# A memory-writing product kernel: VectorE's products in four stretches with fewer waits and counts, even shares, one more border

## The chip, the cores and the metric

The kernel runs on one core of a Trainium2 chip. The time is the device time of one execution in microseconds; a kernel's figure is the median over its runs. Engines are named as the profile names them: DVE is VectorE, ACT is ScalarE, SP is SyncE, POOL is GpSimd. A "q" after an engine's name (DVEq) means its sequencer. A "DMA engine" is one of the core's 16 engines that move the data; a "transfer" is one DMA instruction, whose rows are shared out over all 16.

## The reference

For each row of a 4096 x 256 float32 matrix, all products of two of its elements x_i x_j with i <= j, in the order of the upper triangle's rows:

```python
dot = jnp.einsum('bi,bj->bij', inputs, inputs)
iu, ju = jnp.triu_indices(256)
return dot[:, iu, ju]          # 4096 x 32896 float32
```

The input is 4.19 MB and the output 538.97 MB, so the kernel reads little and writes much.

## The kernel before

Each of the 128 partitions has 32 rows of the input. Two of them (`REPEAT`) are worked on together, so there are 16 groups. A group's 32896 output columns are cut into three thirds (`PIECES`), at columns 10944 and 21920. A piece is one third of one group: 128 partitions x 2 rows x about 10970 columns, and one transfer of 11.2 MB writes it out. Six pieces (two groups) make one pass of the loop (`PASS`), and there are eight passes. Output pieces alternate between two places in the on-chip memory (`PLACES`), so a piece can be computed only when the transfer of the piece two before it has landed.

In a piece, row i of the triangle is the stretch x_i * x_i, ..., x_i * x_255. The piece's first rows go to ScalarE (L206, one activation with a scale for each row i and each of the two input rows), the others to VectorE (L185, one multiplication for both input rows, and mostly for two rows i at once, m = 2 in `vector_ops`, L43). A multiplication with m = 2 writes one element too many, which the next row of the triangle overwrites; therefore that next product must come after it. `split` (L71) chooses how many rows ScalarE gets: it moves rows over until VectorE's planned time is within the third's budget, a number of nanoseconds for each output column of the two rows (`BUDGETS`, L22: 0.95, 0.80 and 0.85), or ScalarE would have more than VectorE.

`interleave` (L57) cuts VectorE's part of a block into two halves and takes products from them in turn. In `vector` (L172) each product goes through `Work.add` (L144): it counts one up on VectorE's own semaphore, and it waits until all products but the last one issued have finished. A product therefore waits for the one two places before it in the order.

The first two pieces are computed ahead of the loop ("ahead"). The very first is cut in blocks at `FIRST` (L23), 512, 1536 and 3584 columns, and each block is sent out as soon as both engines have it; four transfers make up this piece. All other pieces are one block and one transfer. After a block VectorE waits for its own last product and then signals `v_done`; ScalarE waits for its own last instruction and signals `a_done` (L215).

In the loop VectorE first takes `free` of the place (L178, through `take`, L135), which the transfer two pieces before raised by 16 when it landed, then raises `go`, which ScalarE takes (L202). SyncE (L218) takes `v_done` and `a_done` and issues the transfer (L226). All transfers are issued by SyncE, in order. At the start it also issues the three loads of the input (L247).

Of the kernel before, what the change touches and what calls it, by code (L numbers as in the profile page):

```python
# [9 lines left out]
AF = mybir.ActivationFunctionType  # L10
ALU = mybir.AluOpType
# [3 lines left out]
REPEAT = 2  # L15
PIECES = 3
PLACES = 2
PASS = 6
AHEAD = 2


BUDGETS = [0.95, 0.8, 0.85]  # L22
FIRST = [512, 1536, 3584]  # L23


def even_borders(lo: int, hi: int, pieces: int) -> list[int]:
# [30 lines left out]
def interleave(block: list) -> list:  # L57


    half = len(block)  # L60
    while half and len(vector_ops(block[:half])) > len(vector_ops(block[half:])):
        half -= 1
    a, b = vector_ops(block[:half]), vector_ops(block[half:])
    return [op for k in range(max(len(a), len(b))) for ops in (a, b) for op in ops[k : k + 1]]


def vector_time(block: list) -> float:
# [15 lines left out]
def window(ap: bass.AP, free: list) -> bass.AP:  # L83
    return bass.AP(ap.tensor, ap.offset, [list(ap.ap[0]), *free])


@with_exitstack
def kernel(
    ctx: ExitStack, tc: tile.TileContext, x: bass.AP, out: bass.AP
):  # L90

    nc = tc.nc
    n, d = x.shape
    width = out.shape[1]
    each, groups = REPEAT * d, n // (P * REPEAT)
    rounds = PASS // PIECES
    passes = groups // rounds
    assert n % (P * REPEAT) == 0 and width == d * (d + 1) // 2 and width % UNIT == 0
    assert PASS % PLACES == 0 and AHEAD == PLACES and PASS % PIECES == groups % rounds == 0  # L110
    borders = even_borders(0, width, PIECES)
    spans = list(zip(borders, borders[1:]))
    slot = max(b - a for a, b in spans)

    x_in = x.rearrange("(p g) d -> p (g d)", p=P)
    x_out = out.rearrange("(p h q r) c -> h q p r c", p=P, q=rounds, r=REPEAT)

    pool = ctx.enter_context(tc.tile_pool(name="all", bufs=1))
    xt = pool.tile([P, passes, rounds * each], F32, name="x")

    xv = pool.tile([P, each + 1], F32, name="xv")
    xa = pool.tile([P, each], F32, name="xa")
    places = [pool.tile([P, REPEAT, slot], F32, name=f"o{k}") for k in range(PLACES)]
    ctx.enter_context(tc.tile_critical())  # L124

    def semaphore(name: str):
        return ctx.enter_context(nc.semaphore(name))

    free = [semaphore(f"free{k}") for k in range(PLACES)]
    head, v_done, a_done, go = (semaphore(s) for s in ("head", "v_done", "a_done", "go"))  # L130
    loads = [0, each, groups // 2 * each, groups * each]
    loaded = [semaphore(f"loaded{k}") for k in range(len(loads) - 1)]

    def take(engine, sem, value: int):
        engine.wait_ge(sem, value).then_inc(sem, -value)  # L135

    class Work:

        def __init__(self, engine, name: str):
            self.engine, self.sem, self.count, self.marked = engine, semaphore(name), 0, 0

        def add(self, ins, back: int, mark: bool = True):  # L144
            if self.count > back:
                ins._wait_ge(self.sem, self.count - back)
            if mark:
                ins.then_inc(self.sem, 1)
                self.count += 1

        def end(self):
            return self.engine.wait_ge(self.sem, self.count)

        def restart(self):
            self.engine.sem_inc(self.sem, -self.count)  # L155
            self.count = 0

    v, a = Work(nc.vector, "v_own"), Work(nc.scalar, "a_own")

    def x_of(h, q: int) -> bass.AP:  # L160
        return xt[:, bass.ds(h, 1), q * each : (q + 1) * each].rearrange("p o d -> p (o d)")

    def blocks(p: int, ahead: bool):

        lo, hi = spans[p % PIECES]
        cuts = [lo, *(FIRST if ahead and p == 0 else []), hi]
        for a, b in zip(cuts, cuts[1:]):
            block = runs(d, a, b)
            k = split(block, 0.0 if ahead else BUDGETS[p % PIECES] * REPEAT * (b - a))
            yield a - lo, b - lo, block[:k], block[k:], lo  # L170

    def vector(h, pieces: range, ahead: bool):  # L172
        for p in pieces:
            if p % PIECES == 0:
                v.add(nc.vector.tensor_copy(xv[:, :each], x_of(h, p // PIECES)), 0)  # L175
                v.end()
            if not ahead:
                take(nc.vector, free[p % PLACES], 16)  # L178
                nc.vector.sem_inc(go, 1)  # L179
            for _, _, _, block, lo in blocks(p, ahead):  # L180
                for (i, j, at, length), m in interleave(block):
                    at -= lo

                    v.add(
                        nc.vector.tensor_tensor(  # L185
                            places[p % PLACES][:, :, at : at + m * length],
                            window(xv[:, j:], [[d, REPEAT], [1, m], [1, length]]),
                            window(xv[:, i:], [[d, REPEAT], [1, m], [0, length]]),
                            ALU.mult,
                        ),  # L190
                        1,
                    )
                v.end().then_inc(v_done, 1)
        v.restart()

    def scalar(h, pieces: range, ahead: bool):
        for p in pieces:
            if p % PIECES == 0:
                a.add(nc.scalar.activation(xa, x_of(h, p // PIECES), AF.Copy), 0)  # L199
                a.end()  # L200
            if not ahead:
                take(nc.scalar, go, 1)  # L202
            for _, _, block, _, lo in blocks(p, ahead):
                todo = [(run, r) for run in block for r in range(REPEAT)]
                for (i, j, at, length), r in todo:
                    ins = nc.scalar.activation(  # L206
                        places[p % PLACES][:, r, at - lo : at - lo + length],
                        xa[:, r * d + j : r * d + j + length],
                        AF.Copy,
                        scale=xa[:, r * d + i : r * d + i + 1],  # L210
                    )
                if todo:
                    ins.then_inc(a.sem, 1)
                    a.count += 1
                a.end().then_inc(a_done, 1)  # L215
        a.restart()

    def sync(h, pieces: range, ahead: bool):  # L218
        for p in pieces:
            place = places[p % PLACES]  # L220
            parts = list(blocks(p, ahead))
            for lo, hi, *_, base in parts:
                take(nc.sync, v_done, 1)
                take(nc.sync, a_done, 1)
                to = x_out[bass.ds(h, 1), p // PIECES, :, :, base + lo : base + hi]
                nc.sync.dma_start(to.rearrange("o p r c -> p (o r) c"), place[:, :, lo:hi]).then_inc(  # L226
                    free[p % PLACES] if len(parts) == 1 else head, 16
                )

    def all_pieces(engine, pieces_of):  # L230
        pieces_of(0, range(AHEAD), True)
        if engine is not nc.sync:
            for sem in loaded[1:]:
                engine.wait_ge(sem, 16)
        kind = engine.engine
        with nc.Fori(
            0,
            passes,
            engines=OrderedEngineSet([kind]),
            head_slot={kind: 0} if engine is not nc.sync else {},  # L240
        ) as h:
            pieces_of(h, range(AHEAD, PASS), False)
            with engine.If(h < passes - 1):
                pieces_of(nc.s_assert_within(h + 1, 0, passes - 1), range(AHEAD), False)

    for (lo, hi), sem in zip(zip(loads, loads[1:]), loaded):
        nc.sync.dma_start(xt.rearrange("p h d -> p (h d)")[:, lo:hi], x_in[:, lo:hi]).then_inc(sem, 16)  # L247
    nc.vector.memset(xv[:, each:], 0.0)  # L248
    for engine in (nc.vector, nc.scalar):
        engine.wait_ge(loaded[0], 16)  # L250

    take(nc.gpsimd, head, 16 * (len(FIRST) + 1))
    nc.gpsimd.sem_inc(free[0], 16)
    for engine, pieces_of in ((nc.vector, vector), (nc.scalar, scalar), (nc.sync, sync)):
        all_pieces(engine, pieces_of)
    for k in range(PLACES):
        take(nc.sync, free[k], 16)
    for sem in loaded:
        take(nc.sync, sem, 16)
# [27 lines left out]
```

## Time and profile before

| what | value |
|---|---|
| median of 4 runs | 1273.57 us (1273.53 to 1273.59) |
| profiled execution, its own time | 1273.72 us |
| its span, first to last instruction | 1271.7 us |
| VectorE busy | 72% |
| ScalarE busy | 48% |
| DMA written, mean rate | 538.97 MB, 427 GB/s |
| transfers of the output | 51, issued between 6.2 and 1237.5 us |
| SyncE's waits for the two engines | 1231.2 us in 54 waits |

The span is the time from the first to the last instruction of the profile; 2.0 us of the execution lie outside it. In the profile's rows of instruction groups, the columns are line, engine and operation, output and input with their shapes, the count; then busy time and mean duration of one; then the idle time of the engine just ahead of these instructions, and what ended most of it. In the timeline the columns are start, duration, engine, line, operation, shapes and count, with the idle time ahead in brackets. In the rows of stretches the columns are the stretch, the granted clock, busy time and count of each engine, again the clock, the busy share of the DMA engines and their rate.

### The profile page before, as it was taken

The numbers are of one execution on the slowest core, as the hardware profiler recorded it, in microseconds if no ns is written. First come the engines' busy times: TensorE is split into PE (matmuls) and PEld (weight loads), VectorE is DVE, ScalarE is ACT, GpSimd is POOL, SyncE is SP. The second block draws the span as 40 slices with busy tenths as digits, with TensorE's granted clock in tenths as the row PEclk, the third lists the DMA queues.
The fourth block names the chain that finished last, engine by engine and source line by source line (L and its number), as shares of the span: only waits on it lengthen the run. The fifth ranks groups of instructions, "written<-read, shape, count | busy, mean of one in ns | idle before, by whom it ended". The sixth has DMA issues, their size and how long they took to land. (4 is left out here: it accounts for less than half of the span.)

```text
span 1271.7 us, 4308 instructions
## 1 busy us (share of the span) xinstructions
DVE 915.4 (72%) x1712; ACT 606.4 (48%) x1837; POOL 0.2 (0%) x4
## 2 busy tenths in 40 slices
DVE  8767786777768776687757877578776787677860
ACT  8725535254363543635337352473524635156350
POOL 0000000000000000000000000000000000000000
DMA  9999999999999999999999999999999999999998
GB/s 381 435 429 431 439 423 439 422 440 425 435 439 424 437 424 437 423 440 428 435 419 442 419 441 420 431 429 419 442 420 441 420 440 421 420 441 421 440 420 356
DMA packets 14310, 543.21 MB, mean 427 GB/s; under 512 B 864, under 2 KB 864, under 8 KB 1504
## 3 DMA queue, kind: packets, MB, share of 16 engines
q1 hardware_dynamic: 14304, 543.17, 99.3%
q14 instruction: 6, 0.05, 0.0%
HBM read 4.19 MB, written 538.97 MB: 427 GB/s over the span
## 5 line engine op out<-in xcount | busy, mean ns | idle before, releaser
L185 DVE TENSOR_TENSOR o<-xv 128x736 f32<-128x736 f32 (+61 forms) x1695 | 908.5, 624 | 311.6 <-DVEq L135 311.0
L206 ACT ACTIVATE o<-xa 128x198 f32<-128x198 f32 (+44 forms) x1820 | 595.0, 420 | 621.1 <-ACTq L135 620.6
L175 DVE COPY xv<-x 128x512 f32 (+1 forms) x16 | 6.8, 427 | 9.1 <-DVEq L155 4.2
L199 ACT ACTIVATE xa<-x 128x512 f32 (+1 forms) x16 | 10.1, 630 | 5.1 <-ACTq L155 3.4
L199 ACT ACT_TABLE_LOAD x1 | 1.3, 1283 | 4.1 <-DMA x<-in_r_inputs_dram 4.1
L248 DVE MEMSET xv<- 128x1 f32 x1 | 0.1, 59 | 1.0 <-SPq L124 1.0
L274 POOL MEMSET const-bfloat16-1.0<- 128x1 bf16 x1 | 0.1, 102 | 0.0
L274 POOL MEMSET const-uint8-127<- 128x1 uint8 x1 | 0.1, 102 | 0.0
L274 POOL MEMSET const-float32-1.0<- 128x1 f32 x1 | 0.1, 99 | 0.0
L274 POOL MEMSET const-float32-0.0<- 128x1 f32 x1 | 0.1, 98 | 0.2 <-issue 0.2
## 6 DMA issues: line engine op xcount, KB each, us to landing
out_dram<-o SPq DMA_DIRECT2D x32, 10976.0 KB, 33.1
out_dram<-o SPq DMA_DIRECT2D x15, 10944.0 KB, 30.7
out_dram<-o SPq DMA_DIRECT2D x1, 7360.0 KB, 19.9
x<-in_r_inputs_dram SPq DMA_DIRECT2D x1, 2048.0 KB, 12.3
out_dram<-o SPq DMA_DIRECT2D x1, 2048.0 KB, 11.5
x<-in_r_inputs_dram SPq DMA_DIRECT2D x1, 1792.0 KB, 6.8
out_dram<-o SPq DMA_DIRECT2D x1, 1024.0 KB, 9.9
out_dram<-o SPq DMA_DIRECT2D x1, 512.0 KB, 9.3
```

The lines of the kernel that those rows point to most:

```text
L175: v.add(nc.vector.tensor_copy(xv[:, :each], x_of(h, p // PIECES)), 0)
L185: nc.vector.tensor_tensor(places[p % PLACES][:, :, at : at + m * length], window(xv[:, j:], [[d, REPEAT], [1, m], [1, length]]), window(xv ...
L199: a.add(nc.scalar.activation(xa, x_of(h, p // PIECES), AF.Copy), 0)
L206: ins = nc.scalar.activation(places[p % PLACES][:, r, at - lo : at - lo + length], xa[:, r * d + j : r * d + j + length], AF.Copy, scale=x ...
L248: nc.vector.memset(xv[:, each:], 0.0)
L274: nc = _bacc.Bacc("TRN2", target_bir_lowering=False, num_devices=1)
```

## The change

`BUDGETS` becomes 0.85 for all three thirds, and `FIRST` gets a fourth border at 6400, so the first piece goes out in five transfers. `interleave` cuts VectorE's part into four stretches (`SETS`) of about equal numbers of products and takes one from each in turn. With each product it returns the place of the product in the same stretch that has to be finished before it, if that one has m = 2. `vector` adds a wait only where such a product isn't covered by an earlier wait. A wait is for the product two places before or for the one that is needed, whichever is later in the order; and only products that some wait is for, and the block's last, count on the semaphore. ScalarE signals `a_done` with its block's last instruction instead of after a wait for itself, except in the last third of a group, where the wait stays. `go` is no longer taken after each piece: ScalarE's first instruction of a piece waits for the running number of turns, and the semaphore is set back at the end of a call.

```diff
+SETS = 4
...
-BUDGETS = [0.95, 0.8, 0.85]
-FIRST = [512, 1536, 3584]
+BUDGETS = [0.85, 0.85, 0.85]
+FIRST = [512, 1536, 3584, 6400]
...
 def interleave(block: list) -> list:
-    half = len(block)
-    while half and len(vector_ops(block[:half])) > len(vector_ops(block[half:])):
-        half -= 1
-    a, b = vector_ops(block[:half]), vector_ops(block[half:])
-    return [op for k in range(max(len(a), len(b))) for ops in (a, b) for op in ops[k : k + 1]]
+    sets, k = [], 0
+    for left in range(SETS, 0, -1):
+        share = -(-len(vector_ops(block[k:])) // left)
+        end = k
+        while end < len(block) and len(vector_ops(block[k : end + 1])) <= share:
+            end += 1
+        if left == 1:
+            end = len(block)
+        sets.append(vector_ops(block[k:end]))
+        k = end
+    order, last = [], {}
+    for step in range(max(map(len, sets))):
+        for s, ops in enumerate(sets):
+            if step < len(ops):
+                order.append((*ops[step], last.get(s)))
+                last[s] = len(order) - 1 if ops[step][1] == 2 else None
+    return order
...
     def vector(h, pieces: range, ahead: bool):
...
-                for (i, j, at, length), m in interleave(block):
+                order = interleave(block)
+                counted, waits = {len(order) - 1}, {}
+                for k, (*_, before) in enumerate(order):
+                    if before is not None and before > max(waits.values(), default=-1):
+                        waits[k] = max(before, k - 2)
+                        counted.add(waits[k])
+                number = {k: done + 1 + c for c, k in enumerate(sorted(counted))}
+                for k, ((i, j, at, length), m, _) in enumerate(order):
...
+                    if k in waits:
+                        ins._wait_ge(v_own, number[waits[k]])
+                    if k in counted:
+                        ins.then_inc(v_own, 1)
+                done += len(counted)
+                nc.vector.wait_ge(v_own, done).then_inc(v_done, 1)
+        nc.vector.sem_inc(v_own, -done)
...
     def scalar(h, pieces: range, ahead: bool):
...
-            if not ahead:
-                take(nc.scalar, go, 1)
...
-                if todo:
-                    ins.then_inc(a.sem, 1)
-                    a.count += 1
-                a.end().then_inc(a_done, 1)
+                if not ahead:
+                    turns += 1
+                    todo[0]._wait_ge(go, turns)
+                if not todo:
+                    nc.scalar.sem_inc(a_done, 1)
+                elif (p + 1) % PIECES:
+                    todo[-1].then_inc(a_done, 1)
+                else:
+                    todo[-1].then_inc(a_own, 1)
+                    done += 1
+                    nc.scalar.wait_ge(a_own, done).then_inc(a_done, 1)
+        for sem, count in ((a_own, done), (go, turns)):
+            if count:
+                nc.scalar.sem_inc(sem, -count)
```

More of the change, by code (lines that the diff above doesn't have):

```diff
@@ L135, in take @@
         engine.wait_ge(sem, value).then_inc(sem, -value)
[L137 to L158, printed above, removed]
+    v_own, a_own = semaphore("v_own"), semaphore("a_own")
     def x_of(h, q: int) -> bass.AP:
@@ L172, in vector @@
     def vector(h, pieces: range, ahead: bool):
+        done = 0
         for p in pieces:
+            place = places[p % PLACES]
             if p % PIECES == 0:
-                v.add(nc.vector.tensor_copy(xv[:, :each], x_of(h, p // PIECES)), 0)
-                v.end()
+                ins = nc.vector.tensor_copy(xv[:, :each], x_of(h, p // PIECES))
+                if done:
+                    ins._wait_ge(v_own, done)
+                ins.then_inc(v_own, 1)
+                done += 1
+                nc.vector.wait_ge(v_own, done)
             if not ahead:
@@ L180, in vector @@
             for _, _, _, block, lo in blocks(p, ahead):
-                for (i, j, at, length), m in interleave(block):
-                    at -= lo
[L184 to L191, printed above, removed]
-                    )
@@ L193, in vector @@
-                v.end().then_inc(v_done, 1)
-        v.restart()
+                order = interleave(block)
[6 more added lines that the diff above has]
+                for k, ((i, j, at, length), m, _) in enumerate(order):
+                    at -= lo
+                    ins = nc.vector.tensor_tensor(
+                        place[:, :, at : at + m * length],
+                        window(xv[:, j:], [[d, REPEAT], [1, m], [1, length]]),
+                        window(xv[:, i:], [[d, REPEAT], [1, m], [0, length]]),
+                        ALU.mult,
+                    )
+                    if k in waits:
+                        ins._wait_ge(v_own, number[waits[k]])
+                    if k in counted:
+                        ins.then_inc(v_own, 1)
@@ L196, in scalar @@
+                done += len(counted)
+                nc.vector.wait_ge(v_own, done).then_inc(v_done, 1)
+        nc.vector.sem_inc(v_own, -done)
     def scalar(h, pieces: range, ahead: bool):
+        done = turns = 0
         for p in pieces:
+            place = places[p % PLACES]
             if p % PIECES == 0:
-                a.add(nc.scalar.activation(xa, x_of(h, p // PIECES), AF.Copy), 0)
-                a.end()
-            if not ahead:
-                take(nc.scalar, go, 1)
+                nc.scalar.activation(xa, x_of(h, p // PIECES), AF.Copy).then_inc(a_own, 1)
+                done += 1
+                nc.scalar.wait_ge(a_own, done)
@@ L203, in scalar @@
             for _, _, block, _, lo in blocks(p, ahead):
[L204 to L207, printed above, removed]
+                todo = [
+                    nc.scalar.activation(
+                        place[:, r, at - lo : at - lo + length],
                         xa[:, r * d + j : r * d + j + length],
@@ L211, in scalar @@
                     )
-                if todo:
-                    ins.then_inc(a.sem, 1)
-                    a.count += 1
-                a.end().then_inc(a_done, 1)
-        a.restart()
+                    for i, j, at, length in block
+                    for r in range(REPEAT)
+                ]
+                if not ahead:
[7 more added lines that the diff above has]
+                    todo[-1].then_inc(a_own, 1)
+                    done += 1
+                    nc.scalar.wait_ge(a_own, done).then_inc(a_done, 1)
+        for sem, count in ((a_own, done), (go, turns)):
+            if count:
+                nc.scalar.sem_inc(sem, -count)
     def sync(h, pieces: range, ahead: bool):
```

## The prediction

> **What bounds the kernel now.** I read the page's busy times first, then the DMA queues, the waits, the timeline of one pass and the last microseconds.
>
> ```profile
> span 1271.7 us, 4308 instructions
> ...
> DVE 915.4 (72%) x1712; ACT 606.4 (48%) x1837; POOL 0.2 (0%) x4
> ...
> q1 hardware_dynamic: 14304, 543.17, 99.3%
> ...
> L185 DVE TENSOR_TENSOR o<-xv 128x736 f32<-128x736 f32 (+61 forms) x1695 | 908.5, 624 | 311.6 <-DVEq L135 311.0
> L206 ACT ACTIVATE o<-xa 128x198 f32<-128x198 f32 (+44 forms) x1820 | 595.0, 420 | 621.1 <-ACTq L135 620.6
> ```
>
> The 16 DMA engines are full 99.3% of the span. VectorE idles 311 us and ScalarE 621 us, nearly all at L135, where they wait for a place to come free (VectorE) or for the go that follows it (ScalarE). So products are not what the end waits for; the output's transfers are. A change to the engines can gain only where the DMA is not full, or where the engines slow the DMA.
>
> The timeline of one pass shows the rhythm. VectorE starts a piece when the transfer two before it has landed on all 16 engines, so the distance from start to start is the transfer time of the slowest DMA engine.
>
> ```profile
> 1139.76 18.89 DVE L185 TENSOR_TENSOR o<-xv 128x468 f32<-128x468 f32 x60 [8.51 <-DVEq L135]
> 1139.79 18.39 ACT L206 ACTIVATE o<-xa 128x98 f32<-128x98 f32 x62 [13.53 <-ACTq L135]
> ...
> 1166.15 20.75 DVE L185 TENSOR_TENSOR o<-xv 128x996 f32<-128x996 f32 x22 [6.83 <-DVEq L135]
> 1166.21 5.66 ACT L206 ACTIVATE o<-xa 128x256 f32<-128x256 f32 x14 [7.19 <-ACTq L135]
> 1192.20 17.52 DVE L185 TENSOR_TENSOR o<-xv 128x768 f32<-128x768 f32 x24 [5.30 <-DVEq L135]
> 1192.23 12.49 ACT L206 ACTIVATE o<-xa 128x7 f32<-128x7 f32 x36 [20.37 <-ACTq L135]
> 1218.22 18.88 DVE L185 TENSOR_TENSOR o<-xv 128x468 f32<-128x468 f32 x60 [8.50 <-DVEq L135]
> ```
>
> The distances are 26.39, 26.05 and 26.02 us: longest where VectorE runs its 60 short products. The row at 1139.76 also has 18.89 us of work in 18.9 us of wall time: within a piece VectorE has no gap that dropping a wait could close.
>
> The end shows who is slow.
>
> ```profile
> 1264.00:1265.00 1.00, 0.00 (x0) 0.00 (x0) 0.00 (x0) 1.00 1.63 702
> 1265.00:1266.00 1.00, 0.00 (x0) 0.00 (x0) 0.00 (x0) 1.00 0.00 0
> 1266.00:1267.00 1.00, 0.00 (x0) 0.00 (x0) 0.00 (x0) 1.00 0.11 44
> 1267.00:1268.00 1.00, 0.00 (x0) 0.00 (x0) 0.00 (x0) 1.00 0.00 0
> 1268.00:1269.00 1.00, 0.00 (x0) 0.00 (x0) 0.00 (x0) 1.00 0.10 44
> ```
>
> The columns after the clock are DMA share and GB/s; a packet is counted in the slice in which it starts, so rows swing. From 1266 on one packet per slice is left, a single 43.9 KB one: one DMA engine of 16 is still working and the others are done. In the landing records 15 engines finish the last transfer by 1266.65 us and one at 1270.33. That one sets the end.
>
> I followed the landings through the run. From 770 to 1220 us the slow engine needs 26.37, 26.11 and 26.02 us for the transfers that fly while 60, 22 and 24 products are computed. The median engine, in the stretch where it waits for nothing (400 to 560 us), needs 26.03, 25.98 and 25.95. So the slow one loses 0.34, 0.13 and 0.07 us, 0.54 per three pieces. For the last transfer, beside which almost nothing is computed, the slow engine needs 25.95 us, as fast as the others. Its packets say the same: 1627 ns with idle engines, about 1650 with four products per packet, about 1665 with six or seven, about 1631 with two. So it is slowed by what the engines do, and it is the only one.
>
> **The change, part by part.**
>
> *Counts and waits on VectorE.* Counted out of the loops, the loop's three kinds of piece have 60, 22 and 24 products before, each of which counts on VectorE's semaphore and nearly all of which wait. After, they have 61, 20 and 26 products, of which 20, 7 and 9 count and 19, 6 and 8 wait. VectorE itself gains nothing that matters: it is full within a piece already, and a faster piece would only idle longer at L135. What can matter is the slow DMA engine. Two readings of the loss fit the trace. Per product it is 0.34/60 = 5.7 ns, 0.13/22 = 5.9 and 0.07/24 = 2.9: roughly a price for each product. ScalarE's 63, 14 and 36 instructions, which do not count, do not order it that way: a fit over the packets of the second half gives 4.7 ns for each VectorE product that starts in a packet and -0.1 for each ScalarE one. What a product has that a ScalarE instruction lacks is the count (and the wait). If the count is the price, the losses shrink with it: 0.34 x 20/60 = 0.11, 0.13 x 7/22 = 0.04, 0.07 x 9/24 = 0.03. Saved: 0.23 + 0.09 + 0.04 = 0.36 us per three pieces. From the landing of the first piece at about 40.5 us on there are 47 transfers, 15.67 threes: 15.67 x 0.36 = 5.6 us. The trace of before has no product without a count, so this has bounds from both sides: nothing (the product itself is the price; there are as many, 107 for 106), and 15.67 x 0.54 = 8.5 us (with counts this rare the slow engine falls into step with the others). I take 5.6, since the ScalarE rows, instructions without counts, are the nearest to a product without one.
>
> [...]
>
> *Even shares.* The first third's VectorE share falls with its budget, 20.75 x 0.85/0.95 = 18.6 us, and ScalarE gets 22 instructions for 14, 5.66 x 22/14 = 8.9 us. The second third goes to 17.52 x 0.85/0.80 = 18.6 and ScalarE to 12.49 x 32/36 = 11.1. The last third stays. Cost on the path: nothing. What hides it is the transfer in flight: SyncE issues the three transfers 7.9, 6.9 and 4.7 us before the slow engine has finished the one before (second, last, first third). The worst goes to about 6.9, the best to 6.8. Against the 15 others the first third is issued only 0.7 us ahead, which gives them a gap of about 0.5 us; that gap goes, and is worth nothing while the slow engine sets the end. If the cover were gone, each us would be paid in each of 47 transfers.
>
> *One more border.* Now the fourth transfer of the first piece is late:
>
> ```profile
> 21.57 0.37 SPq L226 DMA_DIRECT2D out_dram<-o  x1
> ```
>
> The third has its last packets end around 22, and the fourth's first packets come 0.1 to 0.6 us after them on the engines, 0.35 on average. With the border at 6400 the fourth has 2816 of the 7360 columns: VectorE and ScalarE took 10.2 us for the 7360 (11.2 to 21.4), so about 3.9 for these, and it is issued near 15.3, well ahead. The rest, 4544 columns, is issued near 21.6 as now, while 2816 columns are in flight for some 6.8 us. That takes away 0.35 us and adds one more packet per row: packets of 8192 B take 309 ns, of 29440 B 1093, so 6.7 ns of each don't scale with size, and 16 more per engine are 0.1 us. One more DMA on SyncE takes 0.4 us there, with nothing behind it. Net -0.2 us, between -0.5 and +0.1.
>
> *ScalarE's ends and the cumulative go.* ScalarE's last instruction counts for SyncE directly, without the wait for itself: some 0.05 us per piece under leads of 4.7 us and more. Nothing.
>
> *Sum* against the profiled execution, 1273.72 us (its span of 1271.7 and 2.0 around it): -5.6 -0.2 = 1267.9. That execution lies 0.15 above the median of the runs, 1273.57, so the forecast for a median is **1267.8**. The 0.15 also says that the loss is not one of the profiled execution alone.
>
> **Rivals.**
>
> *The product, not its count, slows the engine.* For it: the price per product holds about as well as the price per count, since before they are the same number, and packets with both engines busy are the worst. Against it: ScalarE's instructions cost next to nothing. A mixture in which every instruction of both engines and every count pay alike: before, 106 products, 112 ScalarE instructions and 106 counts in three pieces, 324; after, 107, 116 and 36, 259. That is a fifth less, 1.7 of the 8.5 us. Then only the border stays: 1273.4, or 1271.7 for the mixture.
>
> *The other DMA engines take over.* If the slow one falls wholly into step, the others' 77.96 us per three pieces set the end: 8.5 + 0.2 less, 1264.9. That is the far end of my forecast, not another sign.
>
> *VectorE gets slower: slower overall.* Four stretches in turn, and products without a wait, may cost each product more. It decides when a piece's products take over about 26 us, the transfer time. The last third has 61 products in 18.9 us and a lead of 6.9 us, so each would have to grow by 6.9/61 = 113 ns. At 125 ns the excess is 0.7 us in each of the 16 last thirds, 11 us: 1285. Against it: the smallest product now takes 153 ns all told, the waits look two products back before and after, and nothing in the rows shows a price of that kind.
>
> **How the numbers follow.** The counted-semaphore case has 0.50, no change (product, or nothing) 0.42, slower 0.08. Within 0.2%, 2.5 us, is about what a measurement of this kernel can tell from no change, so the mixture falls in the second. The range goes from 1264.6 (8.5 and the border's 0.5 off) up to 1273.7 (nothing off, the border at its worst, +0.1), which takes in the no-change case. The likeliest case's own range is 1264.6 to 1271.0. Chances: faster 0.50, same 0.42, slower 0.08.
>
> **What will show it.** Start-to-start distances of VectorE near 26.15, 26.02 and 25.98 for 26.39, 26.05, 26.02; a last DMA engine that ends within 1 to 2 us of the others, for 3.7; the fourth transfer issued near 15 us. If the 60-product distance stays at 26.4 with a third of the counts, the product is the price and my forecast is wrong by the whole 5.6. If VectorE's last third takes well over 19 us, the third rival is under way.

## The result, and the profile after

The changed kernel takes 1272.25 us (median, 1272.05 to 1272.52) against 1273.56 for the one before; the ratio is 0.999, with a 95% interval of 0.9985 to 0.9995. So it is faster by 1.3 us, a tenth of a percent: the sign of the forecast and about a quarter of its size.

The page of the changed kernel, the same parts as before:

```profile
span 1270.0 us, 4343 instructions
...
DVE 896.2 (71%) x1733; ACT 633.9 (50%) x1897; POOL 0.2 (0%) x4
...
q1 hardware_dynamic: 14576, 543.17, 99.4%
...
L189 DVE TENSOR_TENSOR o<-xv 128x752 f32<-128x752 f32 (+62 forms) x1716 | 889.3, 605 | 329.2 <-DVEq L148 328.4
L213 ACT ACTIVATE o<-xa 128x253 f32<-128x253 f32 (+58 forms) x1880 | 622.5, 434 | 591.5 <-DVEq L177 591.4
```

The engines' work has moved a little, from VectorE (908.5 to 889.3 us) to ScalarE (595.0 to 622.5), and both still idle for hundreds of microseconds until a place is free. The DMA is as full as before (99.4% of the span for 99.3). The timeline of one pass (start, duration, instruction group, idle before it):

```profile
1138.23 18.83 DVE L189 TENSOR_TENSOR o<-xv 128x468 f32<-128x468 f32 x61 [7.54 <-DVEq L148]
...
1164.58 18.55 DVE L189 TENSOR_TENSOR o<-xv 128x980 f32<-128x980 f32 x20 [6.85 <-DVEq L148]
...
1190.64 18.46 DVE L189 TENSOR_TENSOR o<-xv 128x776 f32<-128x776 f32 x26 [7.51 <-DVEq L148]
...
1216.66 18.82 DVE L189 TENSOR_TENSOR o<-xv 128x468 f32<-128x468 f32 x61 [7.55 <-DVEq L148]
```

The distances from start to start are 26.35, 26.06 and 26.02 us, where they were 26.39, 26.05 and 26.02. Only the one with the 61 short products has moved visibly, and by hundredths. The end, in stretches of 1 us (the first figure behind a stretch is its length in us; the granted clock stands only once, behind the busy times, and after it DMA share and GB/s):

```profile
1263.00:1264.00 1.00, 0.00 (x0) 0.00 (x0) 0.00 (x0) 1.00 0.10 44
1264.00:1265.00 1.00, 0.00 (x0) 0.00 (x0) 0.00 (x0) 1.00 0.10 44
1265.00:1266.00 1.00, 0.00 (x0) 0.00 (x0) 0.00 (x0) 1.00 0.00 0
1266.00:1267.00 1.00, 0.00 (x0) 0.00 (x0) 0.00 (x0) 1.00 0.10 44
```

One DMA engine is still alone at the end, longer than before: in the landing records the others finish at 1263.25 and it at 1268.69, 5.4 us apart for 3.7. The others have gained 3.4 us, which fits the first thirds no longer coming late for them, and it is worth nothing, as the slow engine sets the end.

For the experiments one number is read from each profile: the time of the slowest DMA engine from landing to landing, as a mean over the transfers from some 460 us on, for the second, last and first third. Its scatter from transfer to transfer is 0.01 to 0.04 us, over ten transfers of each kind. The transfer of a second third is in flight while the next last third is computed, so what is changed in the last third shows in the first of these three numbers. In the first 270 us or so of after, the engine that lands last shows no such price (its transfer beside 61 products takes 25.94 us), so it seems to be another one; the trace does not number the engines. "Products" are VectorE's, "counts" are increments of an engine's own semaphore by its products or instructions (ScalarE's one at the end of a block is left out), all for three pieces in the loop. The medians are of different sets of runs, in which the kernel before took 1273.41 to 1273.57 us, so one or two tenths between rows mean nothing.

| kernel | products | ScalarE instr. | counts | second, last, first third (us) | sum | median (us) |
|---|---|---|---|---|---|---|
| before | 106 | 112 | 106 | 26.375, 26.104, 26.025 | 78.504 | 1273.56 |
| after | 107 | 116 | 36 | 26.328, 26.089, 26.004 | 78.422 | 1272.25 |
| all count | 107 | 116 | 107 | 26.375, 26.111, 26.020 | 78.505 | 1273.60 |
| ScalarE counts | 107 | 116 | 149 | 26.396, 26.122, 26.036 | 78.554 | 1274.42 |
| twice the products | 163 | 116 | 17 | 26.457, 26.065, 26.002 | 78.524 | 1274.86 |
| no VectorE, last third | 46 | 116 | 16 | 26.172, 26.079, 26.004 | 78.255 | 1269.17 |
| little ScalarE, last third | 107 | 56 | 36 | 26.190, 26.087, 26.006 | 78.282 | 1270.11 |
| tiny products, last third | 107 | 116 | 36 | 26.336, 26.081, 26.003 | 78.420 | 1272.31 |
| budgets 1.00, 1.00, 0.95 | 117 | 74 | 39 | 26.308, 26.059, 25.983 | 78.351 | 1270.77 |

### The profile page after: what moved, and what is told of

Read it like the earlier page. It is cut to its first block, busy times and chain, and to the rows that moved or that the text cites. A ratio compares the mean times of both kernels' runs of the same rounds, so it can differ in the third digit from the quotient of the medians.

```text
span 1270.0 us, 4343 instructions
## 1 busy us (share of the span) xinstructions
DVE 896.2 (71%) x1733; ACT 633.9 (50%) x1897; POOL 0.2 (0%) x4
## 3 DMA queue, kind: packets, MB, share of 16 engines
q1 hardware_dynamic: 14576, 543.17, 99.4%
## 5 line engine op out<-in xcount | busy, mean ns | idle before, releaser
L189 DVE TENSOR_TENSOR o<-xv 128x752 f32<-128x752 f32 (+62 forms) x1716 | 889.3, 605 | 329.2 <-DVEq L148 328.4
L213 ACT ACTIVATE o<-xa 128x253 f32<-128x253 f32 (+58 forms) x1880 | 622.5, 434 | 591.5 <-DVEq L177 591.4
```

The source lines that it names most:

```text
L189: ins = nc.vector.tensor_tensor(place[:, :, at : at + m * length], window(xv[:, j:], [[d, REPEAT], [1, m], [1, length]]), window(xv[:, i:] ...
L213: nc.scalar.activation(place[:, r, at - lo : at - lo + length], xa[:, r * d + j : r * d + j + length], AF.Copy, scale=xa[:, r * d + i : r ...
```

## The experiments

"After" in the expectations is the changed kernel, and every edit is to it.

**All products count again.** Is the count the price?

```diff
+                counted = set(range(len(order)))
                 number = {k: done + 1 + c for c, k in enumerate(sorted(counted))}
```

> As after, but every product counts on VectorE's semaphore; waits, order, shares and borders stay. Before and after differ by 70 counts and 0.07 us of the slowest DMA engine's time per three pieces. Theory C (the count is the price): the slowest engine's three transfers are back at 78.50 us for 78.43, and the time at about 1273.4. Theory P (the product instruction itself is the price) or W (the work of the engines is): 78.43 and 1272.25 as after.

Measured: 1273.60 us (1273.38 to 1273.75), ratio to before 1.0001 (0.9992 to 1.001), and a sum of 78.505. The whole gain is gone again with nothing but the counts put back:

```profile
1139.61 18.81 DVE L190 TENSOR_TENSOR o<-xv 128x468 f32<-128x468 f32 x61 [7.58 <-DVEq L148]
1165.99 18.54 DVE L190 TENSOR_TENSOR o<-xv 128x980 f32<-128x980 f32 x20 [6.89 <-DVEq L148]
1192.07 18.46 DVE L190 TENSOR_TENSOR o<-xv 128x776 f32<-128x776 f32 x26 [7.54 <-DVEq L148]
```

VectorE's busy times are those of after to 0.02 us, so the counts cost VectorE nothing; the first distance is 26.38 us. 71 counts for 0.083 us are 1.17 ns each. The waits stay as few as in after, 33 in three pieces where nearly all of the 106 products of before waited, and nothing is left of the gain: it was the counts and not the waits.

**ScalarE counts each instruction.** If a count has a price, it should not matter who counts.

```diff
+                for ins in todo[:-1]:
+                    ins.then_inc(a_own, 1)
+                done += max(len(todo) - 1, 0)
...
+        nc.scalar.wait_ge(a_own, done)
```

> As after, but every ScalarE instruction counts on ScalarE's semaphore, 116 more counts per three pieces. Theory C at 1.0 ns a count: 0.12 us more per three transfers, time 1274.1. Theories P and W: 1272.25.

Measured: 1274.42 us (1274.24 to 1274.72), ratio 1.0008 (0.9999 to 1.0018). 113 counts more are 0.132 us: again 1.17 ns each (by the scatter, both figures are good to 0.1 or 0.2).

```profile
1140.10 18.81 DVE L189 TENSOR_TENSOR o<-xv 128x468 f32<-128x468 f32 x61 [7.62 <-DVEq L148]
...
1166.49 18.54 DVE L189 TENSOR_TENSOR o<-xv 128x980 f32<-128x980 f32 x20 [6.90 <-DVEq L148]
```

The distance is 26.39 us. Theory C is shown for the counts, on either engine.

**Without the border at 6400.**

```diff
-FIRST = [512, 1536, 3584, 6400]
+FIRST = [512, 1536, 3584]
```

> As after, without the border at 6400. If the border is worth what I gave it, the first piece lands 0.2 us later and the time is 1272.45 (0.1 less to 0.5 more at the ends). If the border is the whole of the gain, 1273.5.

Measured: 1272.27 us (1272.15 to 1272.38), ratio 0.9991 (0.9982 to 1.0). The medians are 0.02 us apart, but they are of different runs: against before in its own runs this kernel gains 1.15 us (from 1273.42) and after 1.31. So the border is worth 0.2 us at most, less than these runs can tell from nothing. In the landing records the first piece lands at 41.27 us with it and at 41.72 without, and the last engine ends at 1268.69 and 1268.85. It does what was foreseen in its place, as after issues the fourth transfer 6 us sooner than before:

```profile
15.61 0.37 SPq L245 DMA_DIRECT2D out_dram<-o  x1
```

**Twice the products, same columns.** Does the product itself have a price? In the loop's last thirds VectorE multiplies one row at a time.

```diff
-def interleave(block: list) -> list:
+def interleave(block: list, single: bool = False) -> list:
+    ops_of = (lambda b: [(r, 1) for r in b]) if single else vector_ops
...
-                order = interleave(block)
+                order = interleave(block, not ahead and p % PIECES == 2)
```

> As after, but in the loop's last thirds VectorE multiplies one row at a time, about 117 products for 61 with the same columns; only the block's last counts, none waits. Theory C: 19 counts fewer, the slowest engine's transfer beside the last third goes from 26.32 to 26.30 or less, time 1272 or less. Theory P: the loss of 0.34 us doubles, 26.65, and 16 of these make 1277.5. Theory W (bytes): 26.32, 1272.25.

Measured: 1274.86 us (1274.74 to 1274.97), ratio 1.0011 (1.0002 to 1.002). Neither C, which wants a gain, nor P at its full price.

```profile
1141.07 18.38 ACT L214 ACTIVATE o<-xa 128x98 f32<-128x98 f32 x62 [14.90 <-DVEq L178]
1141.12 22.52 DVE L190 TENSOR_TENSOR o<-xv 128x234 f32<-128x234 f32 x117 [7.54 <-DVEq L149]
...
1167.61 18.54 DVE L190 TENSOR_TENSOR o<-xv 128x980 f32<-128x980 f32 x20 [3.29 <-DVEq L149]
```

The distance is 26.49 us. 56 products more and 19 counts less make 0.129 us; with the counts at 1.17 ns a product costs 2.7. So the product has a price of its own, twice that of its count, and half of what I had put on both together. Of the time, 1.3 us are something else, a late start at the loop's first piece:

```profile
43.65 22.53 DVE L190 TENSOR_TENSOR o<-xv 128x234 f32<-128x234 f32 x117 [5.93 <-DVEq L149]
...
66.58 0.39 SPq L246 DMA_DIRECT2D out_dram<-o  x1
```

It is issued half a microsecond before the fifteenth engine lands the transfer before (67.11 us), and its own transfer takes 27.21 us in the landing records, for 25.95 in after. The price of a product is read from the later transfers and doesn't have this in it. That price leaves much of the loss without an owner, and ScalarE's instructions as the suspects. Theory E: every instruction of either engine and every count has its price.

**VectorE leaves the last third out.** In this run and the next two a part of the output is not computed; the added memset, once ahead of the loop, fills columns that no engine would write.

```diff
+                if not ahead and p % PIECES == 2:
+                    nc.vector.sem_inc(v_done, 1)
+                    continue
                 order = interleave(block)
...
+    nc.vector.memset(places[0][:, :, borders[1] :], 0.0)
```

> As after, but in the loop VectorE leaves its products of the last third out (that part of the output is not computed); ScalarE's 62 instructions stay. The runs so far give 1.17 ns a count and 2.7 ns a VectorE product. Theory E (every instruction and every count has its price, on the slowest DMA engine alone): 61 products and 20 counts less beside the second third's transfer are 0.19 us, 26.33 to 26.14, time 1269.2. Theory B (only both engines working at once slows it): 25.97, time 1266.5.

Measured: 1269.17 us (1269.09 to 1269.36), ratio 0.9967 (0.9954 to 0.998). That is theory E's time; its transfer time is 26.17 for the 26.14 expected, 2.2 ns for a product. Theory B (both engines at once) is out.

```profile
1136.02 18.38 ACT L216 ACTIVATE o<-xa 128x98 f32<-128x98 f32 x62 [14.93 <-DVEq L177]
...
1162.21 8.80 ACT L216 ACTIVATE o<-xa 128x256 f32<-128x256 f32 x22 [6.98 <-DVEq L177]
```

From start to start of ScalarE it is 26.19 us, for 26.36 in after (1138.17 to 1164.53).

**ScalarE leaves most of the last third out.**

```diff
-                    for i, j, at, length in block
+                    for i, j, at, length in (block[:1] if not ahead and p % PIECES == 2 else block)
...
+    nc.vector.memset(places[0][:, :, borders[1] :], 0.0)
```

> As after, but in the loop's last thirds ScalarE computes one row (2 instructions) and leaves the others out; VectorE's 61 products stay. Theory E with the same price for ScalarE's instructions as for VectorE's, 2.7 ns: 60 less are 0.16 us, 26.33 to 26.17, time 1269.6. Theory V (ScalarE's instructions are free, as my fit over the packets of before said): 26.33, 1272.25. Theory B: 25.97, 1266.5.

Measured: 1270.11 us (1269.83 to 1270.15), ratio 0.9974 (0.9963 to 0.9984). Theory V, that ScalarE's instructions are free, is out by 2 us:

```profile
1136.17 0.65 ACT L213 ACTIVATE o<-xa 128x98 f32<-128x98 f32 x2 [14.91 <-DVEq L177]
1136.23 18.82 DVE L189 TENSOR_TENSOR o<-xv 128x468 f32<-128x468 f32 x61 [7.55 <-DVEq L148]
...
1162.43 18.55 DVE L189 TENSOR_TENSOR o<-xv 128x980 f32<-128x980 f32 x20 [6.70 <-DVEq L148]
```

VectorE's row is that of after, 61 products in 18.8 us, and the distance is 26.20. 60 instructions less are 0.138 us, 2.3 ns each: a ScalarE instruction costs what a product does.

**The same number of products, tiny ones.** Is it the number or the bytes?

```diff
+                    if not ahead and p % PIECES == 2:
+                        length = 1
...
+    nc.vector.memset(places[0][:, :, borders[1] :], 0.0)
```

> As after, with the same 61 products, waits and counts in the loop's last thirds, but each writes only one or two elements a row of input (the rest of that part is not computed). Theory E: the slowest engine's transfer stays at 26.33 us, time 1272.25. Theory W (the work, that is the bytes read and written or the busy time): it falls to about 26.14, 1269.2.

Measured: 1272.31 us (1272.05 to 1272.38), ratio 0.9991 (0.9981 to 1.0).

```profile
1138.27 5.56 DVE L191 TENSOR_TENSOR o<-xv 128x4 f32<-128x4 f32 x61 [7.55 <-DVEq L148]
1164.56 8.79 ACT L215 ACTIVATE o<-xa 128x256 f32<-128x256 f32 x22 [7.13 <-DVEq L177]
1164.61 18.55 DVE L191 TENSOR_TENSOR o<-xv 128x980 f32<-128x980 f32 x20 [20.11 <-DVEq L148]
```

61 products that take 5.56 us instead of 18.83 and write next to nothing cost the slow engine as much (26.336 us for 26.328). Neither the bytes of VectorE's products nor their busy time slow it; the number of instructions does: 26.33 us beside the 61 products, full or tiny, and 26.17 with them left out.

**Fewer instructions: larger budgets.** One product of VectorE does two rows for both input rows, which are four ScalarE instructions.

```diff
-BUDGETS = [0.85, 0.85, 0.85]
+BUDGETS = [1.08, 1.08, 1.08]
```

> As after, with budgets of 1.08: VectorE takes more rows, one product of its replacing up to four ScalarE instructions. In three pieces 42 ScalarE instructions for 116, 125 products for 107, 40 counts or so for 36. Theory E: 56 instructions less at 2.7 ns and 4 counts more at 1.17 are 0.15 us, 15.67 times: 2.3 us less, 1270.0. Theory V (only products and counts): 18 products and 4 counts more, 0.8 us more, 1273.1. VectorE's piece takes some 23.7 us, which leaves SyncE about 2 us ahead of the slowest engine, enough.

Measured: 1273.91 us (1273.75 to 1273.97), ratio 1.0004 (0.9995 to 1.0013): a miss by 3.9 us. The price was right, a sum of 78.297 for the 78.27 expected; the time was lost early. In the landing records the first nine transfers after the first piece take 238.1 us, for 234.4 in after, and from there on this kernel is 1.4 us faster. Of the 3.7 us, 1.7 are lost at the first piece of the loop:

```profile
43.68 23.93 DVE L189 TENSOR_TENSOR o<-xv 128x536 f32<-128x536 f32 x69 [5.96 <-DVEq L148]
...
68.01 0.39 SPq L245 DMA_DIRECT2D out_dram<-o  x1
```

It is issued at 68.01 us, when the transfer before has landed on 15 engines by 67.05 and on the last at 67.82: all of them ran dry. VectorE started it at 43.68, though the first piece had landed at 41.13.

**A hand-over by SyncE, and 1.04 for the last third.** I took GpSimd's relay of the first place for the culprit.

```diff
-BUDGETS = [0.85, 0.85, 0.85]
+BUDGETS = [1.08, 1.08, 1.04]
...
-    take(nc.gpsimd, head, 16 * (len(FIRST) + 1))
-    nc.gpsimd.sem_inc(free[0], 16)
...
+        if engine is nc.sync:
+            take(nc.sync, head, 16 * (len(FIRST) + 1))
+            nc.sync.sem_inc(free[0], 16)
```

> Budgets of 1.08, 1.08 and 1.04, and the first place is handed over by SyncE, which waits for the five transfers of the first piece, instead of GpSimd. The kernel with budgets of 1.08 lost its gain, by my reading, where its first piece of the loop was issued at 68.01 us, 1 us after the transfer before had ended: VectorE got the first place 2.7 us after the first piece had landed, by way of GpSimd. Theory E with this reading: no engine runs dry, the slowest engine's three transfers take 78.31 us for the 78.42 of after, the first loop piece is issued near 65, and the time is 1270.5. If the longer pieces lose the gain elsewhere (every pass), 1273.9 again.

Measured: 1272.23 us (1272.01 to 1272.33), ratio 0.9989 (0.998 to 0.9998); sum 78.306 as expected, time 1.7 us above it; again it is the first nine transfers that take 1.7 us longer than in after.

```profile
38.28 28.95 SPq L245 DMA_DIRECT2D out_dram<-o  x2
...
43.47 22.98 DVE L189 TENSOR_TENSOR o<-xv 128x524 f32<-128x524 f32 x68 [5.41 <-DVEq L148]
```

The second of these transfers is issued at 66.84 us, only 0.26 before the fifteenth engine has landed the one before. GpSimd was not the cause: SyncE raises the semaphore at 41.27 and VectorE starts at 43.47 all the same. Its first instruction of the loop is recorded at 43.16, 4.3 us after its branch at the loop's head (38.90; with budgets of 1.08 it is 38.55 to 43.37), and the wait for the place, which comes next, finds the semaphore raised. So it isn't the hand-over that VectorE waits for. What holds it there I have not followed further.

**A smaller last third**, so that this first piece comes in time, in two sizes:

```diff
-BUDGETS = [0.85, 0.85, 0.85]
+BUDGETS = [1.08, 1.08, 0.95]
```

> As after, with budgets of 1.08, 1.08 and 0.95. Where the two kernels with larger budgets lost their gain, the first piece of the loop, a last third, came too late: VectorE starts it at 43.5 us, 2.3 after the first piece has landed, with SyncE's hand-over as with GpSimd's, since its instructions for the loop come only then. With 20.6 us of VectorE it is issued near 64.7, 2.4 us ahead. In three pieces 62 ScalarE instructions for 116, 120 products for 107, 39 counts for 36: 41 instructions less at 2.7 ns, 3 counts more at 1.17. Theory E: 0.11 us less per three transfers, 78.31, and 1.6 us in all, 1270.6. If longer first and second thirds cost something of their own, up to the 1272.2 that the kernel before this one gave.

Measured: 1271.39 us (1271.24 to 1271.59), ratio 0.9983 (0.9974 to 0.9992), between the two values expected; sum 78.331. The next piece, a first third of 1.08, is issued at 91.91 us, 1.1 before the landing on most engines, and the transfer after it lands 0.65 us later than in after: this lead seems to be too short, but no run here took that apart. The first nine transfers take 0.8 us longer than in after, as much as the time lies above the 1270.6 expected.

```diff
-BUDGETS = [0.85, 0.85, 0.85]
+BUDGETS = [1.0, 1.0, 0.95]
```

> As after, with budgets of 1.00, 1.00 and 0.95: 74 ScalarE instructions for 116, 117 products for 107, 39 counts for 36; 32 instructions less. Theory E: 0.08 us less per three transfers, 78.34, 1.3 us in all, 1271.0. SyncE is about 3.5 us ahead of the slowest engine in each piece.

Measured: 1270.77 us (1270.64 to 1270.88), ratio 0.9977 (0.9968 to 0.9986), with a sum of 78.351 for 78.34 expected. It is faster than both kernels, 2.8 us under the one before. VectorE and ScalarE in its page:

```profile
L189 DVE TENSOR_TENSOR o<-xv 128x232 f32<-128x232 f32 (+40 forms) x1869 | 1024.1, 626 | 195.3 <-DVEq L148 194.6
L213 ACT ACTIVATE o<-xa 128x253 f32<-128x253 f32 (+38 forms) x1236 | 401.8, 417 | 806.5 <-DVEq L177 806.4
```

VectorE is busier by 135 us than in after and ScalarE idles for 806: the engines work less evenly, and the kernel is faster; there are 491 instructions less in these two groups.

The four kernels with larger budgets also test the prices together. In the order above they have 42, 48, 62 and 74 ScalarE instructions, 125, 124, 120 and 117 products and 42, 40, 39 and 39 counts in three pieces. With 2.3 ns for a ScalarE instruction, 2.4 for a product and 1.17 for a count, the earlier runs' figures, that makes sums of 78.30, 78.31, 78.33 and 78.35 us, which are the measured ones.

**Relieving the slowest engine by another cut.** In each pass the last 320 columns of the last piece go out by two transfers of their own. That the slowest engine would have less to do by it was a guess: no run shows how the rows of such transfers are shared out.

```diff
+                whole = [(0, P, lo, hi)]
+                if p == PASS - 1:
+                    whole = [(0, P, lo, hi - CARVE), (0, 120, hi - CARVE, hi), (120, P, hi - CARVE, hi)]
+                for p0, p1, c0, c1 in whole:
```

> As after, but in the last piece of each pass the last 320 columns go out in two transfers of their own, one of 120 partitions and one of 8. [...]

Measured: 1277.43 us (1275.9 to 1278.32), ratio 1.0029 (1.0016 to 1.0041): 3.9 us slower than the kernel before in the same runs. Its last microseconds:

```profile
1266.00:1268.00 2.00, 0.00 (x0) 0.00 (x0) 0.00 (x0) 1.00 0.65 194
1268.00:1270.00 2.00, 0.00 (x0) 0.00 (x0) 0.00 (x0) 1.00 0.28 96
1270.00:1272.00 2.00, 0.00 (x0) 0.00 (x0) 0.00 (x0) 1.00 0.11 31
```

The DMA share falls in steps from 1266 on, 0.65, 0.28 and 0.11: several engines end late, not one, where in after 15 have ended by 1263.25. So in this run the work was spread less evenly than in after; that the small transfers did it is a guess. Which engine is the slowest, and whether it can be spared, stays open.

## Why the prediction was right or wrong

*What bounds the kernel:* right. The slowest of 16 DMA engines sets the end in all kernels whose engines don't run dry, and what VectorE and ScalarE do slows it. Leaving out either engine's work in one third moves the whole kernel by 2 to 3 us, though both idle for hundreds.

*The counts:* the mechanism right, the size wrong, and here the prediction failed. I divided the slow engine's whole loss by the products (5.7, 5.9 and 2.9 ns) and took all of it for the count, with "-0.1" ns for a ScalarE instruction from a fit over packets. The runs show 1.17 ns for a count, 2.2 to 2.7 for a product and 2.3 for a ScalarE instruction. 70 counts less are 0.08 us per three pieces, 15.67 times, 1.3 us, for the 5.6 of the sum. The distance beside the last third, 26.39 before, came down to 26.35 and not to 26.15. For the kernel before, the measured prices add up to 0.64 us per three pieces: more than the 0.54 that I set out from, and about what its 78.50 us lie above three times the 25.95 of the last transfer. The fit could not carry what I hung on it: in the last third, where the loss is, ScalarE starts five or six instructions in almost every packet, so there was little to tell its price by, and the smaller losses of the other thirds, 0.13 and 0.07, hang on the baseline of the median engine, which is itself uncertain by some 0.03. The rival that I priced and set aside, every instruction and every count alike, 1271.7, came nearest, and of its kind was the right one.

*The product, not its count, as the price:* half right. The product is the larger part, and it was no part of the change.

*The other engines take over:* didn't happen; they ended 5.4 us ahead.

*VectorE gets slower:* no; 61 products take 18.83 us where 60 took 18.89.

*Even shares:* nothing on the path, as said, though by the prices five instructions more per three pieces cost 0.01 us, 0.2 in all. No run shows that: the kernel with all counts put back ends 0.2 us above the 1273.42 of before in the same runs, but its interval holds zero, and its sum is that of before. The shares were not tried alone.

*The border:* -0.2 us foreseen, between 0 and -0.2 measured, which is within the bounds given and too little to be told from nothing. *ScalarE's ends and the cumulative go:* not tried alone; with all counts put back nothing is left for them to have gained.

*The chances:* 0.42 stood on no change within 0.2%, and that is what came.

## What to carry to other kernels

When the DMA is full, look which of the 16 DMA engines lands last and what its transfers take beside each kind of work; the mean hides it (99.3 and 99.4% of the span here, with one engine 3.7 and 5.4 us behind the others). Here, in recorded runs, instructions and semaphore counts on engines with idle time had a price on it (2.2 to 2.7 ns and 1.17 ns), so fewer and longer instructions won where evener shares didn't (1270.77 us for 1272.25), up to the point where a transfer is issued too late (at 68.01 us with budgets of 1.08, when 15 engines had landed the one before by 67.05). And a price that two suspects share in the trace of before should be split between them, not given to one by a fit in which the other hardly varies.

## What the runs showed of the hardware

In these runs one DMA engine of 16, the one that lands last from some 300 us on, is slowed by about 2.2 to 2.7 ns for each instruction of VectorE or ScalarE and by 1.17 ns for each count of theirs; for VectorE's products the size makes no difference (0.09 us or 0.3 us each). The median one of the 16 isn't slowed: between 300 and 700 us, where it waits for nothing, it takes 26.02 us both beside 61 products and 62 ScalarE instructions and with the products left out.

By which way the slowdown comes was not tried, and one rival is open. Each run has a span and a granted clock beside its time, so, as far as the results tell, some recording was on in all of them. An instruction costs about twice what a count does (2.2 to 2.7 ns for 1.17), as it would if every recorded moment, the start and the end of an instruction and each count, had the one price. Whether a kernel that nothing records pays any of it, no run here shows.

The first piece of the loop starts at 43.5 to 43.7 us, 2.2 to 2.4 us after its place has been handed over (41.27 and 41.26 us), whether SyncE or GpSimd does it; VectorE's first instruction of the loop comes 4.3 and 4.8 us after its branch at the loop's head. What fills that time is open.
